# Query products on quarters of the array, a softmax of two groups at a time on ScalarE, convolution products on ScalarE

## The chip, the cores and the metric

The kernel runs on one core of one Trainium2 chip. A core has TensorE (matmuls, results in PSUM), VectorE, ScalarE, GpSimd (POOL) and SyncE (SP), which here only issues transfers. The engines run side by side, each in its own order, and wait for each other by semaphores. The metric is the device time of one launch in microseconds (us). The kernel before takes 2755.55 us, the median of three runs (2754.53 to 2757.12). The profile is of one more run, 2758.21 us, whose profiled span is 2756.4 us.

## The reference

x is 2 images of 512 channels, 32 x 32 positions, all in fp32. Two layers follow each other; the change lies in the first.

```
xn   = batchnorm(x)
q    = grouped 1x1 convolution of xn: 8 groups of 64 channels
off  = 6x6 depthwise convolution of q, stride 4, padding 1: 8 x 8 places per group
off  = 4 * tanh(1x1(gelu(off + bias)))             # two offsets a place
kv   = bilinear samples of xn at (grid + off)      # 64 sampled places per group
k, v = grouped 1x1 convolutions of kv
pos  = all 1024 positions minus the 64 sampled places, per group
bias = MLP 2 -> 128 -> 128 -> 1 of sign(pos) * log1p(|pos|)
attn = softmax over the 64 places of (q k / 8 + bias)
x    = x + out_w (attn v) + out_b;   x = x + MLP 512 -> 2048 -> 512 (batchnorm(x))
# second layer: attention of all 1024 positions, four 512 x 512 maps, residual
```

## The kernel before

**Names.** A *chunk* is 128 channels of one image, which is two *groups* of 64 channels each; there are 8 chunks and 16 groups. A group's 64 channels are one half of the 128 partitions of its chunk, so `wq` holds for each chunk a 128 x 128 matrix with two blocks of 64 x 64 on its diagonal and zeros elsewhere. `qa` holds the queries of all chunks, 128 partitions by 1024 positions each, and later, in the same place, the attention weights.

**The main loop** computes the bias MLP, by far the most work: 1024 positions x 64 places x 16 groups. It has 256 steps, 16 for each group, each with 4 of the 64 sampled places. In step s

- `st_sum(s - 1, 2)` (VectorE, L546) adds two evicted halves, and GpSimd's accumulating transfer (L548) adds the sum `ub` into `ua` in memory;
- every fourth step SP loads the next table row `fb`, which ScalarE turns into `ta` and `tb` (L494, L501);
- `st_layer1(s + 2)` is one VectorE instruction over 128 x 4096 (L513), the first layer of the MLP;
- `st_layer2(s)` multiplies on TensorE (L530) into four PSUM tiles of two banks from the pool `zp`, which has three such buffers. Each multiplication takes four 32-column tiles of the array side by side. ScalarE evicts each tile (L536 into `rx`, L538 into `ua` or `ub`);
- `st_sum(s, 0)` (VectorE), and every other step `st_layer3` (TensorE, L569) adds 8 places' output to the group's `sim` in PSUM, after step 16 with the product of queries and keys (L560).

**Beside the loop** run two generators, each advanced by at most one `yield` a step; what they emit is placed after the evictions of the step by `tc.issue_after`, so ScalarE and TensorE meet it between two evictions.

- `later()`: `chain(ci)` and `sample(ci)` for the five entries of `CHAINS`, which hold 1, 1, 2, 2 and 2 chunks. Chain 0 runs in the head, before the loop. A chain loads `xn` (SP), normalises it on ScalarE (L189), multiplies it by `wq` (L196, PSUM tile `psq` from `zp`), evicts the queries (L200), and convolves them with 36 taps on VectorE: each tap is a product with a per-partition scalar added into one of three accumulators `acc` (L223, L225), `TAPS[ci]` taps a step. GELU (`gof`), a 1x1 product on two row halves of the array (L242) and tanh follow. `sample` then reads `xn` in a transposed copy from memory and makes keys and values (L329 to L385).
- `softmax_steps(gi)`: for a finished group, ScalarE adds the bias (L581, `ss`), TensorE transposes four squares of 128 into the PSUM tile `pt` of pool `mip` (L585, one buffer), VectorE takes the maximum (L588) and subtracts it (L590), ScalarE the exponential of all 512 elements at once (L592), VectorE the sum (L595), the reciprocal (L596) and the product (L597). After the second group of a chunk the weights are transposed back (L605, two `pb` tiles from `mip`) and copied into `qa` (L608).

Pools of PSUM: `zp` three buffers of two banks, `simp` one bank, `mip` one bank. The order of each engine's instructions is that of the program text and `issue_after`; no planner moves them.

**After the loop** comes `project(0)` and `project(1)` (L742), the attention's output product as seven half-size multiplications each, with what is left of the last groups' softmax (`tail`) between the two, then the MLP (L793) and the second layer (L910, L1008). In the head, `vectors()` makes the small tile `ub` for the second layer, which VectorE copies from PSUM in two instructions (L447, L448).

Of the kernel before, what the change touches and what calls it, by code (L numbers as in the profile page):

```python
# [8 lines left out]
F32 = mybir.dt.float32  # L9
AF = mybir.ActivationFunctionType  # L10
ALU = mybir.AluOpType
AX = mybir.AxisListType
PSUM = bass.MemoryType.PSUM

P = 128
B, C, H, W = 2, 512, 32, 32
HW = H * W
NCH = C // P
DH = 64
J = 64  # L20
# [3 lines left out]
KS = 6  # L24
NG = 16

CHAINS = [[(0, 0)], [(0, 1)], [(0, 2), (0, 3)], [(1, 0), (1, 1)], [(1, 2), (1, 3)]]
HEAD = 3
TAPS = [36, 9, 4, 3, 3]
NU = 4  # L30
# [9 lines left out]
VOFF = {}  # L40
# [8 lines left out]
def conv_seq_kernel(ctx: ExitStack, tc: tile.TileContext, x, xt, kst, cst, vec, wsm, outw, w1, w2, wl, out):  # L49
    nc = tc.nc  # L50
# [9 lines left out]
    def col(name, i=0):  # L60
        return vs[:, VOFF[name] + i : VOFF[name] + i + 1]

    bns = cp.tile([P, 8], F32, name="bns")
    for i, g in enumerate(("bn1g", "bn2g")):
# [21 lines left out]

    zpp, simpp, mipp = (
        tc.tile_pool(name=n, bufs=c, space=PSUM) for n, c in (("zp", 3), ("simp", 1), ("mip", 1))
    )
    zp, simp, mip = zpp.__enter__(), simpp.__enter__(), mipp.__enter__()  # L90
    groups = [(b, k, f) for b in range(B) for k in range(NCH) for f in range(2)]
    with tc.tile_pool(name="lp", bufs=2) as lp, tc.tile_pool(name="ph", bufs=1) as ph:

        def flat(name):
            return zp.tile([P, 2, 512], F32, tag="ps2", name=name).rearrange("p h n -> p (h n)")


        def wake(src, n):
            ps = flat("wake")
            for _ in range(n):  # L100
                nc.tensor.matmul(ps[0:32, 0:512], src[:, 0:32], src[:, 0:512], start=True, stop=True)
# [3 lines left out]
        nc.gpsimd.memset(edge[:, 0:1], -16.0)  # L105
        nc.gpsimd.memset(edge[:, 1:2], -15.5)
        ones = ph.tile([P, 1], F32, name="ones")
        nc.gpsimd.memset(ones, 1.0)
        nc.scalar.activation(ones, ones, AF.Identity)

        for n in range(2):
            idle = lp.tile([P, 4 * HW], F32, tag="h1", name="idle", bufs=3)
            nc.gpsimd.memset(idle[:, 0:512], 0.0)
            wake(idle, n + 1)
        cs = ph.tile([P, 202], F32, name="cs")
        ws = ph.tile([P, 1408], F32, name="ws")
# [8 lines left out]

        def load(ci):
            xn = ph.tile([P, len(CHAINS[ci]), HW], F32, tag="xn", name="xn")
            for i, (b, k) in enumerate(CHAINS[ci]):
                nc.sync.dma_start(out=xn[:, i, :], in_=xv[:, k, b, :])
            return xn  # L130

        xn0 = load(0)
        nc.scalar.dma_start(out=ws[:, P:1024], in_=wsm[:, P:1024])
# [11 lines left out]
        def swap(w, of, n):  # L145
            w = w.rearrange("p (z c) -> p z c", z=4)
            t = ph.tile([P, 10, n], F32, name=f"swap{n}")
            g, ne, a1, a3, keep, t0, t1 = t[:, 0:4], t[:, 4], t[:, 5], t[:, 6], t[:, 7], t[:, 8], t[:, 9]
# [32 lines left out]
        def chain(ci):  # L181
            G = CHAINS[ci]
            K = len(G)
            (b, k0), n = G[0], 128 * K
            xn = xn0 if ci == 0 else load(ci)
            yield
            for i in range(K):
                k = k0 + i
                nc.scalar.activation(  # L189
                    xn[:, i, :], xn[:, i, :], AF.Identity, bias=col("bn1b", k), scale=bns[:, k : k + 1]  # L190
                )
                if ci > 0:
                    yield
                ps = flat("psq")
                for h in range(2):
                    nc.tensor.matmul(  # L196
                        ps[:, h * 512 : (h + 1) * 512], wq[:, k * P : (k + 1) * P],
                        xn[:, i, h * 512 : (h + 1) * 512], start=True, stop=True,
                    )
                nc.scalar.copy(qa[:, b, k, :], ps)  # L200
                yield


            qv = qa[:, b, k0 : k0 + K, :].rearrange("p k (y x) -> p k y x", x=W)


            acc = ph.tile([P, 3, K, 8, 8], F32, tag="acc", name="acc")
            taps = sorted(range(KS * KS), key=lambda t: any(a in (0, KS - 1) for a in divmod(t, KS)))
            for m, t in enumerate(taps):
                (y0, y1), (x0, x1) = ((1 if a == 0 else 0, 7 if a == KS - 1 else 8) for a in divmod(t, KS))  # L210
                ky, kx = divmod(t, KS)
                ys = slice(4 * y0 - 1 + ky, 4 * y1 - 4 + ky, 4)
                xs_ = slice(4 * x0 - 1 + kx, 4 * x1 - 4 + kx, 4)
                a = acc[:, m % 3]

                if y1 - y0 == 8:
                    ops = [(qv.rearrange("p k y x -> p (k y) x")[:, ky - 1 : ky - 1 + 32 * K - 3 : 4, xs_],
                            a.rearrange("p k y x -> p (k y) x")[:, :, x0:x1])]
                else:
                    ops = [(qv[:, i, ys, xs_], a[:, i, y0:y1, x0:x1]) for i in range(K)]  # L220
                for src, dst in ops:
                    if m < 3:
                        nc.vector.tensor_scalar(dst, src, col("dww", t), None, ALU.mult)  # L223
                    else:
                        nc.vector.scalar_tensor_tensor(dst, src, col("dww", t), dst, ALU.mult, ALU.add)  # L225
                if ci > 0 and m % TAPS[ci] == TAPS[ci] - 1:
                    yield
            af = acc.rearrange("p a k y x -> p a (k y x)")
# [200 lines left out]
        def vectors():  # L429
# [11 lines left out]
            for i in range(2):  # L441
                for k in range(NCH):
# [3 lines left out]
                    )  # L446
            nc.vector.tensor_copy(ub[:, 0, :], ps[:, 0:NCH])  # L447
            nc.vector.tensor_tensor(  # L448
                ub[:, 1, :], ps[:, 512 : 512 + NCH], vs[:, VOFF["bp"] : VOFF["bp"] + NCH], ALU.add
            )  # L450
# [23 lines left out]
        NS = NG * NSL  # L474
        tabs, h1s, sums, sims = {}, {}, {}, {}
        evicted, raw = {}, {}
# [100 lines left out]
        def softmax_steps(gi):  # L577
            b, k, f = groups[gi]
            sim = sims.pop(gi)
            ss = f_pool.tile([P, 512], F32, name="ss")  # L580
            nc.scalar.activation(ss, sim, AF.Identity, bias=col("cb3"))  # L581
            yield
            pt = mip.tile([P, 512], F32, tag="mi", name="pt")
            for c in range(4):
                nc.tensor.transpose(pt[:, c * P : (c + 1) * P], ss[:, c * P : (c + 1) * P], ident)  # L585
            ptv = pt.rearrange("p (a j) -> p a j", j=J)
            mx = f_pool.tile([P, 8], F32, name="mx", bufs=2)
            nc.vector.tensor_reduce(mx, ptv, AX.X, ALU.max)  # L588
            ex = sx[:, :, f, :]
            nc.vector.tensor_tensor(ex, ptv, mx.unsqueeze(2).to_broadcast([P, 8, J]), ALU.subtract)  # L590
            yield
            nc.scalar.activation(ex, ex, AF.Exp)  # L592
            yield
            sm = f_pool.tile([P, 8], F32, name="sm", bufs=2)
            nc.vector.tensor_reduce(sm, ex, AX.X, ALU.add)  # L595
            nc.vector.reciprocal(sm, sm)  # L596
            nc.vector.tensor_tensor(ex, ex, sm.unsqueeze(2).to_broadcast([P, 8, J]), ALU.mult)  # L597
            yield
            if f == 0:
                return  # L600
            yield
            for h in range(2):
                pt = mip.tile([P, 512], F32, tag="mi", name="pb")
                for c in range(4):
                    nc.tensor.transpose(  # L605
                        pt[:, c * P : (c + 1) * P], sx[:, 2 * c + h].rearrange("p f j -> p (f j)"), ident
                    )
                nc.scalar.copy(qa[:, b, k, h * 512 : (h + 1) * 512], pt)  # L608
                yield

# [32 lines left out]
        tail = softmax_steps(NG - 1)  # L643
        for _ in range(4):
            next(tail)

# [22 lines left out]
    def multiply(pool, order, product, took):  # L669
        for p in order:  # L670
            ps = pool.tile([P, 2, 512], F32, tag="ps2", name="sw")
            product(ps, *PARTS[p])
            took[p](ps)
# [34 lines left out]
    with tc.tile_pool(name="mp", bufs=1) as mp:  # L708
# [20 lines left out]

        def project(b, parts, wsum):  # L730
            v, q = vp[:, b * NCH : b * NCH + NCH, :], qa[:, b]
# [34 lines left out]
            def o7(ps):  # L766
# [4 lines left out]
            spread(x)  # L771
            multiply(zp, (1, 2, 5, 6, 7, 3, 4), go, {
                1: o1, 2: lambda ps: plus(x11, x11, ps), 5: o5, 6: o6, 7: o7,
                3: lambda ps: plus(x12, x12, ps), 4: lambda ps: plus(x21, x21, ps, ALU.subtract),
            })

# [55 lines left out]
        def layer2(b, p, w, hm):  # L832
# [36 lines left out]
            "p (a k n) -> p a k n", k=2, n=256  # L869
        ))  # L870
        while tail is not None:
            tail = tail if next(tail, 0) is None else None
        xb = normalise(0)
# [3 lines left out]
        load_unit(*units[1])  # L877
        for pl in (mipp, simpp, zpp):
            pl.__exit__(None, None, None)
# [303 lines left out]
```

## Time and profile before

| engine | busy in the span of 2756.4 us | instructions |
|---|---|---|
| TensorE | 2733.9 us, 99% | 20082 |
| VectorE | 2288.8 us, 83% | 1530 |
| ScalarE | 1562.0 us, 57% | 1592 |
| POOL | 369.4 us, 13% | 428 |

| stretch of the span | TensorE busy | VectorE busy | ScalarE busy |
|---|---|---|---|
| 0 to 44 us, head | 39.97 | 18.38 | 14.15 |
| 44 to 2030 us, the loop | 1975.92 | 1878.28 | 1392.11 |
| 2030 to 2063 us, projection | 30.03 | 31.49 | 7.61 |
| 2063 to 2756 us, MLP and second layer | 687.99 | 360.68 | 148.12 |

The busy time of an engine is the time in which at least one of its instructions was at work. TensorE's matmuls are pipelined and overlap, so a mean duration (593 ns for L530) is longer than the distance of their starts; the distance is what counts for its time. A group line of the profile names the line, the engine, the operation, the output and input tiles, the shape, the count, the busy time, the mean of one and the idle time before it with what ended it. Of the small operations that the change touches, the profile has in the whole run: L196 32 records of 618 ns mean; L225 in forms of 49 to 128 elements, means 306 to 442 ns; L588, L590, L595 and L597 16 times each, 678 to 706 ns; L592 16 times, 631 ns, with 7 loads of a function table of 1283 ns; L585 and L605 64 transposes each, 286 and 284 ns.

### The profile page before, as it was taken

What the parts mean: (1) busy time and instruction counts of PE and PEld (TensorE: products, weight loads), DVE (VectorE), ACT (ScalarE), POOL (GpSimd) and SP (SyncE); (2) the same over time, 40 slices, a digit from 0 to 9 for tenths busy, and PEclk for the clock granted to TensorE, in tenths of its full rate; (3) what the DMA queues carried; (4) which work ended last, traced back from release to release, by engine and by line L of the source; (5) the groups of instructions that cost most, each with busy time, mean ns of one, the idle gap of its engine ahead of it and who ended that gap; (6) DMA issues with size and microseconds to landing.
All of it is one profiled execution on the core that took longest, in us unless ns stands there. A gap on an engine that the chain in (4) does not pass through costs nothing.

```text
span 2756.4 us, 46123 instructions
## 1 busy us (share of the span) xinstructions
PE 2733.9 (99%) x20082; PEld 1030.4 (37%) x20082; DVE 2288.8 (83%) x1530; ACT 1562.0 (57%) x1592; POOL 369.4 (13%) x428
## 2 busy tenths in 40 slices
PE   9999999999999999999999999999999999999999
PEld 3335434333433334333333333333334444446455
DVE  5999999999999999999999999999883575466454
ACT  4767767876677766776667667667622122114040
POOL 2111101111111111111111111111152332000000
PEclk9999999999999999999999999999999999999999
DMA  5444444444444434444444444444430111000000
GB/s 180 93 100 93 93 92 85 97 97 93 85 90 95 95 77 92 86 92 93 85 85 95 87 88 93 92 85 92 79 137 31 46 46 46 16 15 0 31 1 31
DMA packets 64681, 214.28 MB, mean 78 GB/s; under 512 B 11104, under 2 KB 13664, under 8 KB 61792
## 3 DMA queue, kind: packets, MB, share of 16 engines
q0 software_dynamic: 36864, 135.28, 26.5%
q1 hardware_dynamic: 26752, 74.98, 7.8%
q8 instruction: 158, 2.59, 0.4%
q10 hardware_dynamic: 864, 1.07, 0.1%
q14 instruction: 43, 0.35, 0.0%
HBM read 71.59 MB, written 6.55 MB: 28 GB/s over the span
## 4 chain that ended last, share of the span: by engine, by line
PE 83%; issue 8%; DVE 6%; ACT 1%; POOL 1%; DMA 0%; DVEq 0%; POOLq 0%; ACTq 0%; SPq 0%
PE ps L530 52%; PE sw L793 14%; PE sw L910 9%; PE sim L569 3%; DVE h L513 2%; PE sw L1008 2%; PE psg L419 1%; POOL ua L548 1%; DVE ub L546 1%; DVE ua L546 1%; DVE xs L750 1%; PE sim L560 0%; DVE acc L225 0%; DMA ua<-ub 0%; PE pkv L345 0%
## 5 line engine op out<-in xcount | busy, mean ns | idle before, releaser
L530 PE MATMUL ps<-h,cw 128*32 128x512 f32 x16384 | 1800.8, 593 | 8.6 <-ACT rx L536 5.5
L513 DVE CUSTOM_DVE_ANT_1 h<-ta,tb 128x4096 f32<-128x4096 f32 (+1 forms) x257 | 1131.7, 4404 | 70.4 <-PE ps L530 67.4
L530 PEld LDWEIGHTS ps<-h,cw 128*32 128x32 f32 x16384 | 587.4, 110 | 1177.6 <-issue 1111.1
L536 ACT ACTIVATE rx<-ps,sc 128x1024 f32<-128x1024 f32 x512 | 569.7, 1113 | 326.1 <-PE ps L530 291.7
L548 POOL DMA_DIRECT2D ua<-ub x254 | 219.4, 864 | 1714.3 <-DVE ub L546 1559.2
L538 ACT ACTIVATE ua<-ps,sc 128x1024 f32<-128x1024 f32 x256 | 308.4, 1205 | 127.2 <-PE ps L530 126.7
L538 ACT ACTIVATE ub<-ps,sc 128x1024 f32<-128x1024 f32 x256 | 308.3, 1204 | 112.0 <-PE ps L530 111.9
L546 DVE SCALAR_TENSOR_TENSOR ua<-rx,sc,ua 128x1024 f32<-128x1024 f32 x256 | 327.5, 1279 | 29.5 <-ACT ua L538 29.3
L546 DVE SCALAR_TENSOR_TENSOR ub<-rx,sc,ub 128x1024 f32<-128x1024 f32 x256 | 327.0, 1277 | 5.8 <-ACT ub L538 5.6
L793 PE MATMUL sw<-xb,w1t 128*128 128x512 f32 x448 | 193.7, 592 | 1.6 <-DVE xs L676 1.6
L793 PE MATMUL sw<-hm,w2t 128*128 128x512 f32 x448 | 193.6, 592 | 0.0
L676 DVE TENSOR_TENSOR hm<-hm,sw 128x1024 f32<-128x1024 f32 x56 | 67.6, 1219 | 112.5 <-PE sw L793 112.3
L569 PE MATMUL sim<-ua,w3s 128*32 128x512 f32 x1024 | 147.8, 595 | 3.0 <-DMA ua<-ub 3.0
L793 PEld LDWEIGHTS sw<-xb,w1t 128*128 128x128 f32 x448 | 85.0, 190 | 109.1 <-issue 105.7
L793 PEld LDWEIGHTS sw<-hm,w2t 128*128 128x128 f32 x448 | 85.1, 190 | 107.1 <-issue 106.4
L676 DVE TENSOR_TENSOR xs<-xs,sw 128x1024 f32<-128x1024 f32 (+1 forms) x48 | 55.4, 1171 | 74.0 <-PE sw L910 36.0
L802 ACT ACTIVATE hm<-hm,vs 128x512 f32<-128x512 f32 x64 | 42.6, 713 | 129.5 <-DVE hm L676 129.5
L910 PE MATMUL sw<-aT,vt 128*128 128x512 f32 x224 | 96.7, 593 | 0.3 <-ACT aT L990 0.3
L494 ACT ACTIVATE ta<-fb,vs 128x512 f32<-128x512 f32 x64 | 88.8, 1387 | 10.7 <-DMA fb<-fdr 10.7
L827 ACT COPY hm<-sw 128x1024 f32<-128x1024 f32 x8 | 8.1, 1010 | 134.9 <-PE sw L793 134.9
L660 POOL TENSOR_TENSOR w1t<-w1t 128x512 f32<-128x512 f32 x32 | 60.5, 1910 | 112.0 <-DMA w1t<-in_w 111.4
L910 PEld LDWEIGHTS sw<-aT,vt 128*128 128x128 f32 x224 | 42.4, 190 | 53.4 <-issue 52.6
(217 smaller groups left out, 1461.5 us busy)
## 6 DMA issues: line engine op xcount, KB each, us to landing
ua<-ub POOLq DMA_DIRECT2D x254, 512.0 KB, 4.6
fb<-fdr SPq DMA_DIRECT2D x64, 512.0 KB, 5.2
w1t<-in_w SPq DMA_DIRECT2D x8, 1024.0 KB, 4.9
w2t<-in_w SPq DMA_DIRECT2D x8, 1024.0 KB, 4.9
xn<-in_x SPq DMA_DIRECT2D x8, 512.0 KB, 5.0
xnt<-in_xt SPq DMA_DIRECT2D x8, 512.0 KB, 5.2
xs<-in_x SPq DMA_DIRECT2D x16, 256.0 KB, 6.4
out<-xs SPq DMA_DIRECT2D x16, 256.0 KB, 2.1
```

The lines of the kernel that those rows point to most:

```text
L494: nc.scalar.activation(ta.rearrange("p j x -> p x j"), fb[:, 0], AF.Identity, bias=col("cb1"), scale=col("w1x"))
L513: nc.vector._custom_dve(TENSOR_ADD_SAT, out=h1[:, y : y + step].rearrange("p y t x -> p (y t x)"), in0=a.unsqueeze(1).to_broadcast([P, ste ...
L530: nc.tensor.matmul(ps[32 * q : 32 * q + 32, h, :], cw2[:, 32 * z : 32 * z + 32], h1[:, 16 * h : 16 * h + 16, q, :], start=True, stop=True,)
L536: nc.scalar.activation(o, ps, AF.Relu, bias=sc[:, 4 + z : 5 + z])
L538: nc.scalar.activation(o, ps, AF.Relu, bias=sc[:, 4 + z : 5 + z], scale=sc[:, z : z + 1])
L546: nc.vector.scalar_tensor_tensor(r[1], r[0], sc[:, z : z + 1], r[1], ALU.mult, ALU.add)
L548: nc.gpsimd.dma_start(out=sums[s][1], in_=sums[s][3], accum_op=ALU.add)
L569: nc.tensor.matmul(sims[gi][q : q + 32, :], w3s[:, 28 - 4 * i : 60 - 4 * i], sums[s + e][z][:, h, :], start=(i == 0), stop=(i == NSL // 2 ...
L660: engine.tensor_tensor(w[o], w[u], w[v], op)
L676: nc.vector.tensor_tensor(out, a, b_, op)
L793: nc.tensor.matmul(ps[:, m, :], w[:, a, k, m * P : (m + 1) * P], x[:, b_, k, :], start=(k == 0), stop=(k == 1),)
L910: nc.tensor.matmul(ps[:, m, :], w[:, a, k, c + m * P : c + (m + 1) * P], x[b_][:, k, :], start=(k == 0), stop=(k == nk - 1),)
```

## The change

- **Query products.** Instead of two multiplications of 128 rows by 128 columns per chunk, four on quarters of the array, 64 by 64: for each group (row half f) and each half of the positions (column half h). Only the two diagonal blocks are multiplied. The result of a quarter lies on the 64 partitions of its position half and in the bank of its group, so ScalarE evicts with four copies of 64 x 512. `xn` holds one chunk instead of K; the second chunk is loaded after the first product.
- **Convolution.** Chain 0 is as before. In chains 1 to 4 ScalarE writes each tap's product into `prod` (12 taps at a time, no adding), 36 instructions for a chain of one chunk and 48 for two, and VectorE sums 12 taps at a time with a reduction. Border rows that some taps don't reach are reduced apart. `prod` is cleared once on GpSimd. `TAPS` sets 6, 6, 4, 4 products a step.
- **Softmax.** For the first group of a chunk only `ss` is written. After the second, eight transposes go into one tile `pt` from `zp`, ScalarE copies all 1024 elements out, VectorE takes the maximum of both groups and negates it, ScalarE does 16 exponentials of 64 elements with the maximum as bias and the sum as a second output, four a step, VectorE takes the reciprocals, ScalarE does 16 scalings, eight a step. The weights go back by eight transposes into one tile of `zp` and one copy. The last two groups are done singly. `mip` is gone and `simp` has two buffers.
- **ub.** The two copies go to ScalarE and GpSimd.
- **End of the loop.** The rest of the last softmax runs between the seven multiplications of `project(0)`, three steps after each, instead of after it.

```diff
-TAPS = [36, 9, 4, 3, 3]
+TAPS = [36, 6, 6, 4, 4]
...
-        tc.tile_pool(name=n, bufs=c, space=PSUM) for n, c in (("zp", 3), ("simp", 1), ("mip", 1))
+    zpp, simpp = (tc.tile_pool(name=n, bufs=c, space=PSUM) for n, c in (("zp", 3), ("simp", 2)))
...
+        prod = ph.tile([P, 12, 2, 8, 8], F32, name="prod")
...
+        nc.gpsimd.memset(prod, 0.0)
...
                 ps = flat("psq")
-                for h in range(2):
+                quads = [(slice(64 * f, 64 * f + 64), slice(64 * h, 64 * h + 64), f, h)
+                         for f in range(2) for h in range(2)]
+                for f_, h_, f, h in quads:
                     nc.tensor.matmul(
-                        ps[:, h * 512 : (h + 1) * 512], wq[:, k * P : (k + 1) * P],
-                        xn[:, i, h * 512 : (h + 1) * 512], start=True, stop=True,
-                    )
-                nc.scalar.copy(qa[:, b, k, :], ps)
+                        ps[h_, f * 512 : (f + 1) * 512], wq[f_, k * P + 64 * f : k * P + 64 * f + 64],
+                        xn[f_, h * 512 : (h + 1) * 512], start=True, stop=True,
+                    )
+                for f_, h_, f, h in quads:
+                    nc.scalar.copy(
+                        qa[f_, b, k, h * 512 : (h + 1) * 512], ps[h_, f * 512 : (f + 1) * 512]
+                    )
+                if i + 1 < K:
+                    xn = load(b, k + 1)
                 yield
...
-                        nc.vector.scalar_tensor_tensor(dst, src, col("dww", t), dst, ALU.mult, ALU.add)
...
+                for m in range(3):
+                    pr = prod[:, :, 0:K] if K == 2 else prod[:, :, m % 2 : m % 2 + 1]
+                    for t in range(12):
+                        for src, dst in pieces(12 * m + t, pr[:, t]):
+                            nc.scalar.activation(dst, src, AF.Copy, scale=col("dww", 12 * m + t))
+                        if t % TAPS[ci] == TAPS[ci] - 1:
+                            yield
...
+                            nc.vector.tensor_reduce(dst, src, AX.X, ALU.add)
...
-            nc.vector.tensor_copy(ub[:, 0, :], ps[:, 0:NCH])
-            nc.vector.tensor_tensor(
+            nc.scalar.copy(ub, ps.rearrange("p (i c) -> p i c", i=2)[:, :, 0:NCH])
+            nc.gpsimd.tensor_tensor(
...
-            pt = mip.tile([P, 512], F32, tag="mi", name="pt")
...
-            nc.vector.tensor_tensor(ex, ptv, mx.unsqueeze(2).to_broadcast([P, 8, J]), ALU.subtract)
...
-            nc.scalar.activation(ex, ex, AF.Exp)
...
+            of = [f] if gi >= NG - 2 else [0, 1][: 2 * f]
+            if not of:
+                return
...
+            pt = flat("pt")
...
+            nc.scalar.copy(
+                e.rearrange("p a f j -> p f a j"), pt[:, 0 : 512 * n].rearrange("p (f a j) -> p f a j", f=n, j=J)
+            )
             yield
...
+            for a in range(8):
+                for i in range(n):
+                    nc.scalar.activation(
+                        e[:, a, i], e[:, a, i], AF.Exp, bias=mx[:, a, i : i + 1], accum_out=sm[:, a, i : i + 1]
+                    )
+                if a % 2 == 1:
+                    yield
...
+            for a in range(8):
+                for i in range(n):
+                    nc.scalar.activation(e[:, a, i], e[:, a, i], AF.Copy, scale=sm[:, a, i : i + 1])
+                if a % 4 == 3:
+                    yield
...
-            multiply(zp, (1, 2, 5, 6, 7, 3, 4), go, {
...
+            for p in (1, 2, 5, 6, 7, 3, 4):
+                multiply(zp, (p,), go, took)
+                between()
```

## The prediction

> **What bounds the kernel now.** I read the page first: the busy shares, the 40 slices and the chain that ended last.
>
> ```profile
> PE 2733.9 (99%) x20082; PEld 1030.4 (37%) x20082; DVE 2288.8 (83%) x1530; ACT 1562.0 (57%) x1592; POOL 369.4 (13%) x428
> PE   9999999999999999999999999999999999999999
> DVE  5999999999999999999999999999883575466454
> ACT  4767767876677766776667667667622122114040
> PE 83%; issue 8%; DVE 6%; ACT 1%; POOL 1%; DMA 0%; DVEq 0%; POOLq 0%; ACTq 0%; SPq 0%
> L530 PE MATMUL ps<-h,cw 128*32 128x512 f32 x16384 | 1800.8, 593 | 8.6 <-ACT rx L536 5.5
> ```
>
> TensorE is busy from end to end at full clock, so only two things change the time: fewer or shorter TensorE instructions, and fewer gaps between them. The gaps are small. A busy PE is modelled, so I also took the starts of its matmuls from the trace: L530 starts four column tiles together every 429 ns, and whatever exceeds that stream is a stall. Such stalls sum to about 16 us in the loop (44 to 2030 us), about 5 around its end, about 9 in the head.
>
> Next the busy time in three stretches of 60 us, a chain of two chunks beside the loop (first two) and none (third). Columns: us, then PE, PEld, DVE, ACT, POOL busy with counts, clock, DMA share, GB/s.
>
> ```profile
> 360.00:420.00 60.00, 59.08 (x538) 21.06 (x534) 59.97 (x72) 40.21 (x37) 6.02 (x7) 1.00 0.41 92
> 660.00:720.00 60.00, 58.27 (x538) 17.92 (x533) 59.94 (x71) 39.69 (x37) 5.96 (x7) 1.00 0.38 81
> 1500.00:1560.00 60.00, 60.00 (x564) 18.31 (x560) 55.36 (x26) 41.38 (x38) 6.97 (x9) 1.00 0.44 89
> ```
>
> With a chain, VectorE has no idle time and TensorE loses 0.9 and 1.7 us. ScalarE stays at 40 of 60 everywhere. A clean step is 7.295 us of TensorE (68 rounds of 4 in two steps, 14.59 us), against 6.73 of VectorE (4.341 + 2 x 1.196, by starts), a slack of 0.56, and 4.2 of ScalarE plus 0.43 for tables, a slack of 2.7.
>
> The waits of TensorE and ScalarE in the loop (us, times, longest):
>
> ```profile
> PE ps L530 <- ACT rx L536: 5.5, 7, 1.7
> PE sim L569 <- DMA ua<-ub: 3.0, 4, 0.9
> PE ps L530 <- DVE kvz L359: 1.0, 1, 1.0
> ACT rx L536 <- DVE ub L546: 28.2, 12, 4.0
> ```
>
> By place, from the starts: .84, .83 and 1.89 at 208, 458 and 713 us, where ScalarE itself waits for a late VectorE (the last row); 3.67 on L569, whose accumulating transfer went out late because its sum ub was late; 1.13 for kvz. VectorE's lateness is 8.4 us together. The other L530 stalls (.78, .81, .95, .53 = 3.1 us) follow bursts of small ScalarE work between the eviction of ub and that of the next rx. One of them in order of time:
>
> ```profile
> 582.50 1.29 ACT L329 ACTIVATE wt<-th,hb 128x128 f32<-128x128 f32 x4
> 583.80 1.28 ACT L592 ACT_TABLE_LOAD   x1
> 585.09 0.63 ACT L592 ACTIVATE sx<-sx 128x512 f32<-128x512 f32 x1
> 585.63 1.10 ACT L536 ACTIVATE rx<-ps,sc 128x1024 f32<-128x1024 f32 x1
> 586.78 1.50 PE L530 MATMUL ps<-h,cw 128*32 128x512 f32 x12 [0.65 <-ACT rx L536]
> ```
>
> Bursts of 2.96, 3.00, 3.14 and 3.42 us cost .78, .81, .53 and .95. So a burst up to about 2.2 us is free, and beyond it each us costs a us of TensorE.
>
> **The Trainium skill.** *TensorEngine Tiling (Array Packing)*, Key Properties, says that different tiles run in parallel and that a change of mode drains the engine. The trace agrees: pairs of L242 on two row halves start 7 ns apart, and a switch into the transposes costs 94 ns, back 93. Its PSUM Bottleneck section warns that tiling doesn't speed the eviction; that is so here. *ScalarE: Activation LUTs*, What ACT_TABLE_LOAD costs, prices an ACTIVATE at 186 ns + 0.833 an element, 93 for a pointer operand, 93 overlapped. The trace agrees: 128 elements (L329) start 292 ns apart, and the load takes 1283. *SBUF — State Buffer*, Door 1, says that accesses crossing to a new 16-byte line pay a penalty; the trace's L225, which reads every fourth float, rises by 1.87 ns an element.
>
> **The change, part by part**, against the span of 2756.4 us. The three runs' median, 2755.55, is 0.85 lower, and I apply the sum to it.
>
> *Quarter products.* L196 before is 4 records a chunk at 430 ns apart, 1.72 us. After: 8 records, 4 side by side, 2 x 429 = 0.86. That no run of before shows four quarters at once is the unknown: from 0.86 (rows and columns pack, as L242 and L530 each do) to 8 x .43 = 3.44. I take 0.86: in 7 chunks of the loop 7 x .86 = **-6.0**. ScalarE evicts in 4 copies of 64x512, about .58 each (2.3), where one of 0.93 served. The second chunk's xn now loads into the same buffer after the first product, on SP's queue; the transfer takes 5.0 us, a step 7.3, so it is hidden.
>
> *Convolution.* VectorE loses 36 (first chain: one chunk) or 48 (two chunks) taps; by starts 335 ns for 112 elements, 358 for 128, 8.2 and 13.4 us a chain. It gains reductions over 12 products: bounds 4.9 (the rate of a contiguous reduce) to 8.8 (L225's strided rate), so it is 4.6 to 8.5 us lighter per two-chunk chain. Each L513 and L546 in that time is less late. Ceiling 8.4, floor 0; I take **-6**, since what is left comes in lumps of 1.6 to 2.9 us per reduce, and only 0.56 of slack a step works them off. ScalarE gains as many small instructions at about .29 (64 elements) to .40 (128): nearest rows L329 and the skill's price. The 1.5 us memset on POOL is in the head before any use. Chain 0 stays on VectorE.
>
> *Softmax.* Per chunk VectorE drops 2 x (.602 + .601 + .596 + .12 + .602) = 5.04 and takes about 1.4 (maximum of 1024 and negation): -3.6, part of the 6 above. ScalarE takes one copy of 1024 (.95), 16 exponentials with accumulated sum (about .24 + .093 each), 16 scalings (.24), spread over six steps: 10 to 12 us more in 32 steps, 0.35 a step against 2.7 of slack. Table loads fall from 20 to 18 in the program. The transposes are as many, but 29 insertions in the loop become 15; each costs entry 94, exit 93, first record 57, 0.244 us: **-3.4**.
> The transposes now take one of the three PSUM buffers of L530. When ScalarE copies late, L530 waits one buffer earlier; that is inside the next price.
>
> *ScalarE's bursts.* I laid the program's order of ScalarE out by hand with these pitches. Places over 2.2 us between evictions that reach 2.9: 3.7 (12 products and one more, step 43), 4.1 (6 products and 7 scalings, step 44), 3.5 (step 50), 3.2 (copies of psq and pb, step 77), 3.0 (step 105). Their excess is 1.5 + 1.9 + 1.3 + 1.0 + .8 = 6.5; the old 3.1 goes: **+3.4**. Every place over 2.2 together makes 9; I count only those above 2.9, 0.72 of it, since one wait also moves the next burst into its slack. With all small instructions lengthened to .30 the list gives 16, to .40 32, to .50 54, of which 0.72 is 12, 23 and 39. Bounds: -3 (all hidden) to +20.
>
> *ub's copies* (L448, one on VectorE to ScalarE, one to POOL): L530's start at 43.7 us waits 2.2 for them. psq's .86 less and 1.4 more of eviction cancel out: **-0.3**, bounds ±1.5. *End of the loop*: the last tails run between products of project(0). Before, L742, L605 and the first L793 stalled .75 to 1.72 there, 5 us in all; pb's single buffer goes, but ScalarE's scalings come late: **0**, ±3.
>
> Sum: -6.0 - 6 - 3.4 + 3.4 - .3 = -12.3, and one insertion fewer after the loop (three before, two after) -.2: -12.5. **2755.55 - 12.5 = 2743**.
>
> **The rivals.**
> *Everything on ScalarE hides* (its mean of 40 of 60 speaks for it; the four stalls after bursts speak against): -6.0 - 8.4 - 3.6 - 3.1 - .3 = -21.4, 2734.
> *VectorE's relief is not worth anything*, since reductions come in lumps and the late transfers stay: -12.5 + 6 = -6.5, 2749. For it: the slack of 0.56 a step is less than the shortest reduction. Against: VectorE's 59.97 of 60, from which 4.6 us or more is taken.
> *ScalarE becomes the wait* in the chains of two chunks. Place: the evictions of rx in the 9 steps of the products. The gains without the new bursts are 6 + 6 + 3.6 + .3 + 3.1 = 19, so by the list above it decides from about .37 us for each small instruction. At .5 (reads at a stride of 16 bytes, accumulator reads) 39 - 19 = +20: 2775. For it: the strided L225 costs VectorE nearly twice a contiguous read. Against it: L329, .292 with 128 elements.
> *The quarters do not run side by side* by rows: 8 records x .43 = 3.44 a chunk, +1.72 x 7 = 12 instead of -6: 2761. L242's pairs speak against it.
>
> **How the numbers follow.** Forecast .60, all hidden .15, no relief .12, ScalarE the wait .08, quarters in turn .05. The range 2734 to 2755 leaves out the two slow cases (.13) and a little of the fastest. The likeliest case alone: 2738 to 2749. About 0.2% (5.5 us) is what a measurement here tells from no change. Faster by more: the forecast less .05 at its upper edge, all hidden, and half of "no relief", .76; slower: the last two cases less a little, .10; within: the rest, .14.
>
> **What the profile would show.** Quarters: eight records a chunk, two rounds 0.43 apart. Taps: no strided VectorE product after the first chain, reductions of 1.6 to 2.9 us, VectorE about 56 of 60 at 360 us. L530's waits for rx in place of those for VectorE: under 7 us in the loop right, over 20 wrong. Transposes into zp in 17 insertions. Small ScalarE instructions .24 to .40 apart; at .45 or more the forecast fails, and so it does if accumulator reads cost far over .093 or if a copy of the transposes keeps L530's buffer over 3 us.

## The result and the profile after

The changed kernel takes **2742.86 us** (median of 4 runs, 2741.46 to 2744.24) against 2755.53 beside it: ratio 0.9953, 95% interval 0.9936 to 0.9971. The forecast was 2743 us, a change of -12.5. The total came out, but as a sum of terms several of which were wrong, and that they cancelled was luck. So most of what follows is about the terms.

The page of the kernel after, the lines that answer to those of before:

```profile
PE 2721.3 (99%) x20114; PEld 975.2 (36%) x20114; DVE 2248.2 (82%) x1327; ACT 1686.6 (61%) x2164; POOL 374.7 (14%) x430
...
DVE  6999999998999899999999999999774574466454
...
PE 91%; DVE 4%; issue 2%; ACT 2%; DMA 1%; SPq 0%; POOL 0%; DVEq 0%; ACTq 0%; POOLq 0%
...
L565 PE MATMUL ps<-h,cw 128*32 128x512 f32 x16384 | 1790.9, 593 | 7.1 <-ACT rx L571 4.8
```

TensorE is still the bound (layer 2 is L565 now, layer 3 L604). The three stretches of 60 us:

```profile
360.00:420.00 60.00, 58.21 (x536) 17.31 (x532) 55.23 (x28) 55.13 (x94) 6.03 (x7) 1.00 0.39 82
660.00:720.00 60.00, 60.00 (x564) 18.25 (x560) 57.85 (x30) 51.16 (x69) 6.88 (x8) 1.00 0.44 89
1500.00:1560.00 60.00, 60.00 (x560) 18.57 (x556) 55.53 (x27) 42.53 (x46) 6.88 (x8) 1.00 0.43 89
```

VectorE, at 59.97 and 59.94 of 60 before, has 55.23 and 57.85; ScalarE, at 40, has 55 and 51. TensorE has become whole at 660 us, and at 360 us is worse than before. Its waits in the loop, and one of ScalarE's, say why:

```profile
PE ps L565 <- ACT rx L571: 4.8, 4, 2.5
PE ps L565 <- ACT ua L573: 1.5, 1, 1.5
PE sim L604 <- DMA ua<-ub: 0.2, 1, 0.2
ACT ta L529 <- DMA fb<-fdr: 7.1, 2, 3.6
```

The wait on the accumulating transfer, 3.0 us before, is 0.2: VectorE's sums are in time. The last line is new: ScalarE waits for the table `fb`, and what waits behind it on ScalarE is an eviction.

**Where the time went.** I cut each profiled span at the end of the first and the last eviction of `ub` and at the first product of the MLP. Durations in us:

| kernel | head | loop | after the loop | MLP and layer two | span |
|---|---|---|---|---|---|
| before | 54.13 | 1952.60 | 56.89 | 692.81 | 2756.44 |
| after | 51.22 | 1936.34 | 62.10 | 692.80 | 2742.46 |
| difference | -2.9 | -16.3 | +5.2 | 0.0 | -14.0 |

The loop gave more than forecast, and the stretch behind it took a part back. TensorE's own time between the first and last record of layer 2, added up from start to next start, shows what kind it is: products of queries 13.31 to 7.13; transposes 16.89 to 14.85; layers 2 and 3 1904.90 to 1896.05. Of the last, 4377.75 rounds at 0.42917 us make 1878.8 in both. The rest is 26.1 before and 17.3 after; at 0.114 us for each of 52 and 41 insertions of other work (the median distance that an entry adds in both traces), 20.2 and 12.6 us are stalls. I use these sums below, as they leave nothing out.

One thing lies across these figures. The profile of before (2758.21 us) holds a stretch of lower TensorE clock at 44.66 us that costs 1.7 us, in the head by this cut; its runs near the median don't have it, as their mean clock of 1.000 shows. The profile of after (2744.24 us) holds three such stretches before its last part, one in the loop and two behind it; the mean clock is 0.998 in all four runs of this kernel, so the others have about as many. The last section shows them.

### The profile page after: what moved, and what is told of

Its sections match the earlier page's. It is cut to its first block, busy times and chain, and to the rows that moved or that the text cites. A ratio compares the mean times of both kernels' runs of the same rounds, so it can differ in the third digit from the quotient of the medians.

```text
span 2742.5 us, 46612 instructions
## 1 busy us (share of the span) xinstructions
PE 2721.3 (99%) x20114; PEld 975.2 (36%) x20114; DVE 2248.2 (82%) x1327; ACT 1686.6 (61%) x2164; POOL 374.7 (14%) x430
## 4 chain that ended last, share of the span: by engine, by line
PE 91%; DVE 4%; issue 2%; ACT 2%; DMA 1%; SPq 0%; POOL 0%; DVEq 0%; ACTq 0%; POOLq 0%
PE ps L565 58%; PE sw L850 14%; PE sw L967 9%; PE sim L604 4%; PE sw L1065 2%; DVE h L548 2%; PE sw L796 1%; PE psg L454 1%; DVE ua L581 0%; PE sim L595 0%; DVE ub L581 0%; DMA fb<-fdr 0%; PE pkv L380 0%; DMA ua<-ub 0%; ACT rx L571 0%
## 5 line engine op out<-in xcount | busy, mean ns | idle before, releaser
L565 PE MATMUL ps<-h,cw 128*32 128x512 f32 x16384 | 1790.9, 593 | 7.1 <-ACT rx L571 4.8
L565 PEld LDWEIGHTS ps<-h,cw 128*32 128x32 f32 x16384 | 535.4, 110 | 1224.0 <-issue 1170.2
L604 PE MATMUL sim<-ua,w3s 128*32 128x512 f32 x1024 | 135.5, 594 | 0.2 <-DMA ua<-ub 0.2
L245 ACT ACTIVATE prod<-qa,vs 128x56 f32<-128x56 f32 (+4 forms) x180 | 64.0, 440 | 0.0
```

The lines of the kernel that those rows point to most:

```text
L245: nc.scalar.activation(dst, src, AF.Copy, scale=col("dww", 12 * m + t))
L565: nc.tensor.matmul(ps[32 * q : 32 * q + 32, h, :], cw2[:, 32 * z : 32 * z + 32], h1[:, 16 * h : 16 * h + 16, q, :], start=True, stop=True,)
L604: nc.tensor.matmul(sims[gi][q : q + 32, :], w3s[:, 28 - 4 * i : 60 - 4 * i], sums[s + e][z][:, h, :], start=(i == 0), stop=(i == NSL // 2 ...
```

## The experiments

The loop and the stretch after it are cut as above; all kernels not said otherwise start from the changed one, and the diffs are shortened, with words in place of longer pieces. The kernel before ran beside each group, with medians from 2755.56 to 2756.45 us; the changed kernel wasn't run again, so differences of about 1 us against it are not settled.

**Full products again (run e1).**

```diff
-    four matmuls of 64x64 (quads) and four copies of 64x512
+    for h in range(2): matmul of 128x128 into ps[:, 512h:512h+512]
+    nc.scalar.copy(qa[:, b, k, :], ps)
```

> The changed kernel with the two full 128x128 query products and one copy of 128x1024 put back (everything else stays). Theory (the quarters are worth what their records say): the psq records in the loop take 13.3 us instead of 7.1, so the time rises by about 6 us over the changed kernel, to 2749. Rival (ScalarE's four copies of 0.58 in place of one of 0.93 give part of it back in bursts): the stalls of L565 for rx fall by 1 us or more when the single copy returns, and the time rises by 4 or less.

Measured: 2749.66 us (0.9976 of before, 0.9966 to 0.9985), +6.8 against the changed kernel. The records of psq in the loop are back at 13.31 us, +6.2. The stalls are 13.1 us in place of 12.6; without the rounds at lower clock in both (2.8 and 1.7 us) 10.3 in place of 10.9, so the single copy brings back at most 0.6 us. The theory holds. The products before, then the quarters in the changed kernel and their eviction:

```profile
L196 PE MATMUL psq<-xn,ws 128*128 128x512 f32 x32 | 15.9, 618 | 0.4 <-ACT xn L189 0.4
```

```profile
L198 PE MATMUL psq<-xn,ws 64*64 64x512 f32 x64 | 8.7, 614 | 0.4 <-ACT xn L190 0.4
L203 ACT COPY qa<-psq 64x512 f32<-64x512 f32 x32 | 18.5, 578 | 1.5 <-PE psq L198 1.2
```

Twice the records of before take about half the busy time: four start 7 ns apart, the next four 0.43 us later. The eviction, in four copies a chunk, keeps ScalarE busy for 18.5 us where one copy a chunk took 8.1 (L200).

**Convolution on VectorE again (e2).**

```diff
-TAPS = [36, 6, 6, 4, 4]
+TAPS = [36, 9, 4, 3, 3]
-    chains 1 to 4: products on ScalarE into prod, tensor_reduce
+    all chains: scalar_tensor_tensor on VectorE, tap by tap
```

> The changed kernel with the taps of all chains on VectorE again, 9, 4, 3 and 3 a step as before; quarters, softmax on ScalarE and the rest stay. Theory (the convolution is what made VectorE late; ScalarE's products cost about 4 us of bursts, and the chains that became longer cost about 6 us by late table loads at 270 and 512 us): the stalls of layer 2 and 3 behind VectorE return, 14 or more us, ScalarE's 10 us go, so the time rises by 3 to 6, to about 2747. Rival 1 (the softmax had given VectorE the slack already): the late stalls stay away and the time falls by 6 to 10 us, to 2734. Rival 2 (the convolution is worth all of the relief and ScalarE's products cost nothing): +12 or more.

Measured: 2747.12 us (0.9970 of before, 0.9960 to 0.9981), +4.3; the loop +3.5. VectorE is full again, and TensorE waits for late sums:

```profile
360.00:420.00 60.00, 58.11 (x530) 19.97 (x526) 59.97 (x63) 42.00 (x59) 6.01 (x7) 1.00 0.36 77
...
PE sim L578 <- DMA ua<-ub: 3.7, 4, 0.9
```

The line for `fb` is gone from ScalarE's waits. Placed one by one, about 12 us of TensorE's stalls stand behind VectorE in this run, against about 1 us in the changed kernel; the late tables (6.2 us) and most of the stalls after ScalarE's bursts are gone. So the convolution on ScalarE is worth 3.5 us net in the loop: it removes far more lateness than that and brings waits of its own.

**The old softmax (e3).**

```diff
-    softmax_steps: both groups after f == 1, on ScalarE; pt and pb in zp
+    softmax_steps as before; pool mip; simp one buffer
-    project(0, ..., three tail steps after each product)
+    project(0, ...); then the rest of the tail
```

> The changed kernel with the softmax of before (one group at a time, subtraction, sum and scaling on VectorE, one exponential of 512 on ScalarE, its own PSUM bank), and its last part after project(0) as before; quarters, convolution on ScalarE and ub stay. Theory (softmax in one pass saves 2.7 us of transposes' insertions in the loop and some of VectorE's lateness, but loses about 5 us in the end of the loop): the loop is 3 to 6 us longer, the stretch from the last L565 to the first product of the MLP 5 us shorter, the total within 2 us of the changed kernel. Rival (the end of the loop is longer for another reason, ub or the order of the products): the stretch stays at 64 us and the total is 3 to 6 longer.

Measured: 2747.01 us (0.9968, 0.9955 to 0.9981), +4.2. The loop is 7.7 us longer, more than the 3 to 6 expected, and the total is not within 2 us: transposes +2.1, twelve more insertions, stalls 17.2 against 12.6. Of these stalls only about 2 us stand behind VectorE; the waits for late tables, which are in this run too, grew by 0.9 us, and the rest I haven't divided. The stretch after the loop is 56.92 us, that of before, at full clock; so its lengthening comes from the new softmax and its place, not from the rest of the change.

**Both undone: quarters, one `xn` and `ub` alone (e11).**

> Quarters, one xn and ub alone: convolution on VectorE and softmax as before, with the order after the loop as before. Theory (parts add up): the loop is that of before, 1961.1, less 6.2 to 6.6 us, 1954.7; by the two single undoings (+3.7 and +8.0 on 1944.1) it would be 1955.8; the head is 2 us shorter, the stretch after the loop 58.8; the time about 2747 to 2748. Rival (convolution and softmax take the same lateness of VectorE away, so undoing one alone leaves most of it hidden): undoing both costs over 14 us, and the loop is 1958 or more.

Measured: 2752.62 us (median of 20; 0.9987, 0.9980 to 0.9994). The loop is 12.2 us longer than the changed one's; the two single undoings make 3.5 + 7.7 = 11.2. The parts of the loop add up nearly. The time misses its forecast by 5 us; that forecast took the loop from the profile of before, whose stretch of lower clock (1.7 us) the median run of before doesn't have, and this run's own profile, at 2751.27, lies below its median. Against before this loop is only 4.1 us shorter where psq alone takes 6.2 less: after the first step the stalls are 20.6 us against 18.5, about 15 of them behind VectorE. Step by step, in each chain of two chunks TensorE gains about 1.7 us in the eight steps with the products and gives 0.9 to 1.0 back in the next eight, where VectorE is full. In this loop a shorter TensorE is worth its whole only where VectorE has slack.

**The first chain in four steps (e5).** In the changed kernel chain 1 takes two steps more than before and chain 2 one fewer, so their ends come two steps and one step later (loop steps 28 and 59 instead of 26 and 58); nothing in the forecast counted steps. `fdr` is written by the chain's last step and read back as `fb`. SyncE's transfers around the end of the first chain, before and then after:

```profile
252.18 2.54 SPq L289 DMA_DIRECT2D fdr<-fe  x4
254.89 13.76 SPq L484 DMA_DIRECT2D fb<-fdr  x2
```

```profile
260.72 2.54 SPq L324 DMA_DIRECT2D fdr<-fe  x4
263.37 7.80 SPq L519 DMA_DIRECT2D fb<-fdr  x2
```

The write comes 8.5 us later, though the loop by then runs about 5.5 us ahead; together that is 14 us, two steps. And the wait that follows from the second chain's late table, on ScalarE and then TensorE:

```profile
511.86 1.27 ACT L529 ACTIVATE ta<-fb,vs 128x512 f32<-128x512 f32 x1 [3.60 <-DMA fb<-fdr]
512.94 0.68 ACT L536 ACTIVATE tb<-fb,vs 128x512 f32<-128x512 f32 x1
513.52 1.09 ACT L571 ACTIVATE rx<-ps,sc 128x1024 f32<-128x1024 f32 x1
...
514.66 4.91 PE L565 MATMUL ps<-h,cw 128*32 128x512 f32 x28 [2.54 <-ACT rx L571]
```

```diff
-TAPS = [36, 6, 6, 4, 4]
+TAPS = [36, 9, 6, 4, 4]
-    if t % TAPS[ci] == TAPS[ci] - 1: yield
+    if (12 * m + t if ci == 1 else t) % TAPS[ci] == TAPS[ci] - 1: yield
+    (chain 1: the sum over a dozen is issued one step behind its products)
```

> The changed kernel with the products of the first chain of the loop (one chunk) spread over four steps of nine instead of six of six, as many steps as before the change; each sum stands one step behind its last products. Theory (the chains became longer in steps, so the tables of groups 2 and 4 are written to memory and read back too late; ScalarE waits for them in front of the next eviction): ScalarE's two waits for fb, 7.1 us, and TensorE's stalls at 270 and 512 to 518 us (6.2 us together) go, nine products of 0.29 cost at most 0.4 a step in four steps: -4.5 to -6 us, to about 2738. Rival (the late tables come from a late transfer, contention or VectorE, not from the number of steps): the stalls stay, 2742 to 2744.

Measured: 2738.82 us (0.9936, 0.9922 to 0.9951), -4.0; the loop -3.8. ScalarE has no wait for `fb` left, and the stalls at 270 and 512 us are gone. It is a little under the expected, since nine products beside the tables cost 0.9 us in each of two places (179 and 206 us), more than the 0.4 allowed. The number of steps was the cause.

**The burst law (e8 and e9).** The prediction charged each burst of small ScalarE work between two evictions with its excess over about 2.2 us. Two tries at shortening bursts, both on the shortened first chain.

```diff
+    (e8: also two tail steps a product of project(0))
-    scalings: yield at a % 4 == 3
+    scalings: yield at a % 2 == 1
```

> As the run with both, and the scalings of a chunk four a step (four steps) instead of eight a step (two). Theory (a burst over about 2.2 us between two evictions costs its excess): the stall at 387 us after six products and seven scalings (4.2 us, it cost .83) goes, the one at 378 (twelve products and one scaling, it cost 1.3) stays or shrinks to 1.1; about -1 us against the run with both in the loop. Rival (bursts cost by the steps in which they stand, not by their length): the stall is split in two of half the size, no gain.

```diff
-    if tail is not None: issue after evicted[s][s % 4 == 0]
+    if tail is not None and s % 4: issue after evicted[s][0]
```

> The first chain of the loop in four steps (as in the run e5), and no step of a softmax in every fourth loop step, where it stands behind the same eviction as the chain's products because the tables take the other place. The order after the loop is that of the changed kernel. Theory (a burst over about 2.2 us between two evictions costs its excess; at 364 us twelve products and four exponentials, 4.7 us, cost 1.5, at 395 six products and the copy of pb, 3.5 us, cost .9): both stalls shrink, the loop of 1940.2 us in e5 becomes 1937.5 to 1938.5, and the time 2736 to 2737.5. Rival (ScalarE is behind for several steps there, so the work only moves): the loop stays within 0.7 us of 1940.2.

Measured: e8 2738.76 us, loop 1933.46; e9 2738.27, loop 1932.28; the loops of their bases, e7 (the next experiment) and e5, are 1932.73 and 1932.57. Neither gained; three profiles of the same loop code (after, e4 and e6) differ by 0.8 us, and both differences lie within that. e8 doesn't test its theory: the stall at 387 us that it aimed at was no longer there in its base, where the scalings stand in other places. The edit put four of them behind six products at 392.81 us, a burst of 3.7 us that cost 1.7 where six products and the copy of pb had cost 1.1. In e9 the stalls at 364 and 395 us did shrink (1.67 to 1.39 and 1.0 to 0.5), but new ones of 0.3 to 0.9 us stand at 373, 411, 418 and 659 us: the work moved, as the rival has it. And the twelve products alone, 3.4 us, cost 1.39 at 364 us, where with four exponentials behind them, 4.75 us, they had cost only 0.28 more. The bursts of the changed kernel show why the sum of lengths misleads:

```profile
375.14 3.48 ACT L245 ACTIVATE prod<-qa,vs 128x49 f32<-128x49 f32 x12
378.53 0.33 ACT L651 ACTIVATE sx<-sx,sm 128x64 f32<-128x64 f32 x1
378.77 1.10 ACT L571 ACTIVATE rx<-ps,sc 128x1024 f32<-128x1024 f32 x1
...
383.18 2.59 ACT L245 ACTIVATE prod<-qa,vs 128x112 f32<-128x112 f32 x6
385.66 1.78 ACT L651 ACTIVATE sx<-sx,sm 128x64 f32<-128x64 f32 x7
387.33 1.11 ACT L571 ACTIVATE rx<-ps,sc 128x1024 f32<-128x1024 f32 x1
```

The first burst is 3.63 us long (375.14 to 378.77) and cost 1.31, as 2.2 us of slack has it. The second is 4.15 and cost only 0.83. TensorE's instructions of the same places tell them apart:

```profile
373.46 5.33 PE L565 MATMUL ps<-h,cw 128*32 128x512 f32 x48
379.92 0.64 PE L565 MATMUL ps<-h,cw 128*32 128x512 f32 x4 [1.12 <-ACT rx L571]
381.66 1.04 PE L604 MATMUL sim<-ua,w3s 128*32 128x512 f32 x8
382.51 5.33 PE L565 MATMUL ps<-h,cw 128*32 128x512 f32 x48
388.49 1.92 PE L565 MATMUL ps<-h,cw 128*32 128x512 f32 x16 [0.65 <-ACT rx L571]
```

Ahead of the second burst stands a visit of layer 3, two rounds or 0.86 us in which TensorE needs no eviction: the slack is about 3.1 there. The same holds at 364 us: with the exponentials a visit of layer 3 lies beside the burst, in e9 it lies behind it. That fits the four costs (1.4, 1.1, 1.7 and 1.2 worked out; 1.31, 0.83, 1.67 and 1.39 measured); no run isolates it, so it is not shown.

**Fewer tail steps between the products (e4; e7 with the chain of e5).**

```diff
-    lambda: [next(tail, None) for _ in range(3)]
+    lambda: [next(tail, None) for _ in range(2)]
```

> The changed kernel with two steps of the last softmax after each multiplication of project(0) instead of three, so that its transposes back (pb) stand after the fifth product on TensorE instead of the fourth. Theory (TensorE waits 3.5 us at 2004 to 2009 for ScalarE's scalings, which end only then): the wait of pb goes, and the time falls by 2 to 4 us, to about 2740. Rival (the stretch is bound by VectorE's sums, L804 and L730, on which the first product of the MLP waits): the wait of pb goes but comes back at the products of project(1), and the time stays within 1 us.

> The first chain in four steps and two steps of the last softmax after each product of project(0). If both theories hold they add up, as they lie 1500 us apart: -4.5 to -6 and -1.7 us, about 2736 to 2737. If one of them only moves a wait, less than that.

Measured: 2741.13 us, -1.7 (before 2755.56, ratio 0.9945, 0.9928 to 0.9961); with the first chain in four steps as well 2737.97, -4.9. The wait of pb went, but waits of 2.4 and 1.4 us for VectorE's sums took its place, so the stretch is 59.17 us; that is between theory and rival. How large the gain is stays unsure: the four profiles with three steps and one stretch of lower clock after the loop, as this run has it, have 59.7 us, only 0.5 more. The two edits together gain 0.8 less than their sum, within the spread of the runs.

**`ub` on VectorE again (e6).**

```diff
-    nc.scalar.copy(ub, ...); nc.gpsimd.tensor_tensor(ub[:, 1, :], ...)
+    nc.vector.tensor_copy(ub[:, 0, :], ...); nc.vector.tensor_tensor(ub[:, 1, :], ...)
```

> The changed kernel with ub written by VectorE in two instructions as before. Theory (those two stood in front of the first layer's second half on VectorE, for which the first L565 waited): the first L565 starts about 2 us later, near 43.7 us, and the time rises by 2 us. Rival (the head is shorter by the quarters of chain 0): the first L565 starts at 41.5 to 42 us and the time does not change.

Measured: 2743.54 us, +0.7 by the medians where 2 was expected, within the spread of either. The first L565 starts at 44.44 us instead of 41.62:

```profile
PE ps L565 <- DVE ub L483: 2.6, 1, 2.6
```

The end of the first eviction of ub moves by 1.9 us (53.15 against 51.22). So the wait is that of the instruction, as the theory has it; how much of it reaches the end isn't settled by four runs.

**A version from these (e10).** The chain in four steps, no tail step in every fourth step, and for the last group alone the old softmax in the old order, its transposes in the second buffer of `simp`.

```diff
+    def softmax_last(gi): (the function of before, pt and pb from simp)
-    tail = softmax_steps(NG - 1); next(tail)
+    tail = softmax_last(NG - 1); four times next(tail)
-    project(0, ..., between)
+    project(0, ...)
```

> As e9, and the last group alone has the softmax of before in the order of before: bias, maximum, subtraction and one exponential ahead of project(0), the rest after it; its transposes are in the second bank of the group outputs. Theory (the stretch after the loop is longer because ScalarE's sixteen small instructions and VectorE's maximum, which now waits behind project's sums, come before the transposes back, and TensorE, after waiting for them, is granted a lower clock): the stretch from the last L565 to the MLP is 58.8 us as before the change instead of 61.5 to 64, the time falls by 2.5 to 4 against e9, to about 2733. Rival (the stretch is long because VectorE is bound by POOL's work beside it): it stays at 61 or more.

Measured: **2735.62 us** (0.9925 of before, 0.9909 to 0.9942), 7.2 below the changed kernel. The stretch after the loop is 57.63 us, against 59.70 in e9. The gain over e9 is 2.7 us, as expected, though the stretch stays 0.7 above that of before. In the profiles 1.7 of the 2.1 us are the lower clock, which e9's has once in this stretch and this version not at all, so by itself the order is worth 0.4 us.

## Why the forecast came out, point by point

- **The bound and the method** held. TensorE was and is busy to the end, the MLP and the second layer took 692.8 us in both, and the gain came from fewer rounds and fewer stalls.
- **Quarters**: -6.0 forecast, 6.2 in the records, 6.8 by the time when undone. The unknown was whether rows and columns pack at once. They do: eight records, two rounds.
- **Insertions**: -3.4 in the loop forecast. Measured 2.0 in the transposes' records and 1.25 in eleven fewer entries from layers 2 and 3: 3.3.
- **Prices**: small exponentials start 239 ns apart plus 93 for the accumulator read, scalings 239, products 277 to 422 (forecast .24, .093 and .29 to .40). The Trainium skill, *ScalarE: Activation LUTs*, What ACT_TABLE_LOAD costs, gives 186 + 53 + 93 - 93 = 239 for 64 elements and one pointer operand; the trace agrees to the nanosecond. Reductions of 12 products took 1.56 to 2.95 us against bounds of 1.6 to 2.9. The rival in which ScalarE becomes the wait, from .37 us an instruction on, did not occur: only 72 of the products lie above.
- **VectorE's relief**: the term was -6, with a ceiling of 8.4, and it failed by size. The ceiling summed the prediction's list of long waits. Over all starts the loop before has 20.2 us of stalls: 1.7 are the lower clock at the very start, 3.2 follow bursts, 2.0 are small pieces, and 13.3 stand behind VectorE. What the list lacked is at layer 3, which waited 8.4 us for late sums where the list has 3.7; the rest are shorter waits in the same stretches of the loop and in two more places. After, of 12.6 us, 6.2 are late tables, 3.6 bursts, 0.9 the first step, 0.8 small pieces and 1.1 stand behind VectorE. The relief is about 12 us, twice the term. It is the convolution's: about 12 us are back with that alone undone, about 2 with the softmax alone undone, about 15 with both.
- **ScalarE's bursts**: +3.4 forecast, as 6.5 new less 3.1 old. The prices were right, and so were four of the five places: at steps 43, 44, 77 and 105 stalls stand, but they cost 1.3, 0.8, 0.3 and 0.7 instead of 1.5, 1.9, 1.0 and 0.8. At step 50 there is none instead of 1.3; 0.2 each stand at 41 and 49. So the new ones cost about 3.6, net nearly nothing. What failed is the slack of 2.2 us taken as the same everywhere; already the four bursts from which it was drawn give 2.2, 2.2, 2.6 and 2.5.
- **The step that was missing**: the change moves the ends of the chains by steps. It was costed by durations alone, though the numbers in `TAPS` and the steps for each sum say that chain 1 has two steps more. Late tables cost 6.2 us of stalls, 1.7 of them a stretch of lower clock after the wait at 514 us, and 4.0 us came back by giving the two steps back.
- **Head**: -0.3 forecast; the first eviction of ub ends 2.9 us earlier. I had TensorE's wait of 2.2 us for the copies, but let psq's smaller terms cancel it. The lower clock in the profile of before, 0.69 in the mean from 45 to 50 us, is 1.7 of the 2.9, so the change itself brought about 1.2.
- **After the loop**: 0 forecast, bounds ±3; +5.2 in the profile. Sixteen small instructions, a maximum that waits behind VectorE's work for `project`, and the scalings all precede pb:

```profile
2006.29 0.95 PE L660 MATMUL pb<-kp,sx 128*128 128x128 f32 x2 [1.94 <-ACT sx L651]
```

  This profile has two stretches of lower clock there, 3.4 us together, so 1.8 of the 5.2 is the order. With the same code the stretch is 59.7 us in four other profiles (e1, e2, e5, e9), each with one such stretch, and 62.1 in e6, with two; from these the order costs 1.1 to 1.8 us. The term of 0 left out the clock, and its bounds of ±3 were too narrow.

Added up by what was measured: quarters -6.2, insertions -3.3, VectorE -12.2, small pieces -1.2, bursts +0.4, tables +6.2, head -1.2 and after the loop +5.2 make -12.3; the medians say -12.7. VectorE's relief, the bursts and the head came out about 11 us better than forecast, the tables and the stretch after the loop about 11 us worse. That the two sums met is luck; nothing in the forecast ties one to the other.

## What to carry to other kernels

Work that is spread over a loop in steps has a deadline in steps: when an edit changes how often it yields, count the steps to whoever reads its result, DMA round trip included, before adding up durations. Take stalls as a sum over all starts less the bare rounds, not as a list of the large gaps: the list in the prediction names 11.4 us of 20.2, and 4.8 of what it lacks was VectorE's. And a gain on the bounding engine shrinks where a second engine is nearly full: the quarters brought 6.2 us beside a relieved VectorE and 4.1 beside a full one.

## What the runs showed of the hardware

The granted clock of TensorE falls to half after some waits, for 3.41 us at a time (in e1 once for 6.83), and each such stretch costs up to 1.7 us. Averages over 5 or 10 us blur this to 0.69 or 0.83. The stretches of the kernel after up to the MLP, then the one of the kernel before (the clock is the third number from the end):

```profile
514.82:518.24 3.42, 3.42 (x20) 0.85 (x17) 3.14 (x2) 3.39 (x5) 0.00 (x0) 0.50 0.97 229
...
2006.45:2009.86 3.41, 3.30 (x10) 1.95 (x10) 3.38 (x3) 1.46 (x7) 3.36 (x3) 0.50 1.08 411
...
2026.93:2030.34 3.41, 3.41 (x5) 1.35 (x5) 1.22 (x1) 3.41 (x6) 0.00 (x0) 0.50 0.00 0
```

```profile
44.66:48.08 3.42, 3.42 (x24) 1.07 (x20) 3.25 (x1) 1.12 (x1) 0.00 (x0) 0.50 0.56 230
```

From 515.4 to 518 us the rounds of layer 2 start 0.85 us apart instead of 0.43. The four stretches follow waits of TensorE of 2.5 us (for the late table), 1.9 (for pb), 2.8 (for VectorE) and 2.2 (for `ub`). Of the kernel before, 23 runs beside the last experiments lie at 2754 to 2757 us with a mean clock of 1.000 and at 2757 to 2758 with 0.999, which fits one such stretch more. After the loop, eight of the nine profiles with the new tail have one or two, and none of the four with the old order has one (before, e3, e10, e11). But the run with two tail steps and the shorter chain (e7) waited 2.4 and 1.9 us there at full clock, and e10 3.2 us. What decides it stays open.
